# Row sums and differences made in the convolution stage, and a forward transform folded twice along x

## The chip, the cores and the metric

The kernel runs on one core of a Trainium2 chip. The metric is the device time of one launch in microseconds (us); below it is given as the median of the runs. Where a span is named, it is the time from the first to the last instruction of one profiled execution.

## The reference

The input x has 16 images of 16 channels of 256 x 256 numbers, all float32. Two layers follow each other:

```python
x = x + _L0_conv_ref(_gn(x), L0_conv_weight)
x = x + _L1_conv_ref(_gn(x), ty, tx, weights_pole1, weights_pole2, weights_residue)
```

`_gn` normalizes groups of two channels of an image to mean 0 and variance 1. The first layer is a circular 3 x 3 convolution over the 16 channels, written with Fourier transforms in the reference; v is its result with x added. The second layer is a Laplace neural operator:

```python
alpha = jnp.fft.fft2(x, axes=(-2, -1))
A = 1.0 / (omega1[:, None, None, None] - weights_pole1[None])
Bm = 1.0 / (omega2[:, None, None, None] - weights_pole2[None])
S = jnp.einsum('ikpq,oikp,xikq->oxik', weights_residue, A, Bm)
output_residue1 = jnp.einsum('biox,oxik->bkox', alpha, S)
C = jnp.einsum('biox,oikp->bikpx', alpha, A)
D = jnp.einsum('bikpx,xikq->bikpq', C, Bm)
output_residue2 = jnp.einsum('bikpq,ikpq->bkpq', D, weights_residue)
x1 = jnp.fft.ifft2(output_residue1, ...).real
...
x2 = jnp.einsum('kbiqz,biqx->kizx', F, E2).real
return x1 + x2 / Nx / Ny
```

So the spectrum alpha of each image is mixed over the channels at each frequency and transformed back (x1), and 4 x 4 projections of it onto the poles, for each image and channel, are expanded as exponentials (x2). The result is v + x1 + x2/(Nx Ny).

## The kernel before

The kernel goes through four stages; between them, data lies in scratch in HBM.

**Convolution** (order written by hand: the stage is under a manual schedule). The partitions hold four bands of 32 (r = 0 to 3) of the image's rows, each band with 2 rows times 16 channels; bands 2 and 3 hold the lower half of the image. `load_x` (L107) brings half an image as one transfer of 128 partitions, on SP's queue, into one of five buffers. `conv(g)` (L216) issues one round of 16 products of 32 x 32 (L230): four column positions c times four bands r. Six rounds make a unit u of a band, four units an image, and bands 2 and 3 run three rounds behind bands 0 and 1. When a unit is full, ACT evicts it to a buffer vt (L248, five buffers), SP stores it to vD (L252), and the sums for the group norm of the second layer are taken by ACT (L256) for odd bands and by DVE's bn_stats (L263) for even ones. Bands 2 and 3 are mirrored when they are evicted, so that the store has rows y and 255 - y side by side, lower and upper half of vD[b]. Two further strands run beside it, one step at a time: `x_stats` (L146) makes the weights and biases of the next image, with a due time for each step counted in rounds before the image starts; and the tables of the second layer (`make_hat` L319, `make_exps` L394, `make_c` L438, `make_coef` L373) are made by generators, one step every 2 or 5 rounds (L549 to L570), on all engines.

**Statistics of v.** `v_stats` (L265) runs after the last round, for all 16 images at once: DVE steps, two small products on PE, a root on ACT. It gives vmr, the mean and the inverse deviation for each image and channel.

**Forward** (L578 to L703; its order is made by the scheduler from the program's loops). A unit is one channel i and four images. `fold` (L597) loads the two halves of v with four transfers on SP (L601), makes their sum and difference s on POOL (L605, L606; 1024 elements each), and folds s along x into vf on DVE: L610 (four instructions of 128 elements, with the mean added), L613 (512) and L614 (1024). `lines` (L617) transforms along y: sixteen products of 128 x 128 x 256 (L623, L631), with vf as the weights; ACT evicts them to t, four times 768 elements (L639). `columns` (L647) makes the projections psd (L652) and the transform along x, ps_x: four products of 128 x 128 x 512 with the cosine and sine tables (L663). ACT copies the odd half to q (L666); DVE combines even and odd half into spec (L669 to L672, one input from PSUM); small parts are set by ACT (L675) and POOL (L676). After four units, spec (4096 KB) goes to aD on ACT's queue (L690), and the projections are multiplied by their coefficients on DVE (L702) and added up on POOL (L703). The pools of the stage are opened in the order b_const, vy, fold_y, fold_x, lines, sines, spec, prod.

**Mix** (L708 to L942, manual schedule). The constants ct (from cD, 4096 KB), p2k, kgrp and mcol are loaded on SP (L735 to L742); DVE makes the weights of a group (L754 to L780), POOL spreads them (L783), PE sums over poles (L805), and PE mixes channels (L863), with the spectrum loaded from aD (L849) into abd, which POOL sets to zero at first (L907). Results go to yD.

**Inverse** (L945 to L1039, order made by the scheduler). For each output channel and four images: POOL folds yk into u (L993), PE transforms back (ps_p L1018, ps_h L1007, ps_f L1023 and L1024), ACT copies the second half of ps_f to q (L1026). For each image DVE makes sum and difference r of the halves (L1028, L1029), and folds r out along x into ol (L1030, L1031, both inputs in SBUF); then it adds v, loaded as vl (L1034, 2048 elements), and the result is stored on ACT's queue.

A float32 product is two PE instructions in the profile.

Of the kernel before, what the change touches and what calls it, by code (L numbers as in the profile page):

```python
# [16 lines left out]
B = 16  # L17
# [7 lines left out]
def conv_then_laplace_kernel(ctx: ExitStack, tc: tile.TileContext, a: dict, out: bass.AP):  # L25
# [28 lines left out]
    trig = const("trig", [P, 2, P])  # L54
# [31 lines left out]
    nc.vector.tensor_copy(tabE[:, 0], trig[:, 0])  # L86
    nc.vector.tensor_copy(tabO[:, C], trig[:, 1])
# [10 lines left out]
    vp = p1.enter_context(tc.tile_pool(name="vt", bufs=5))  # L98
    sp = p1.enter_context(tc.tile_pool(name="stats", bufs=2))
    sw = p1.enter_context(tc.tile_pool(name="setup", bufs=1))  # L100
    sa = p1.enter_context(tc.tile_pool(name="v_stats", bufs=1))
# [5 lines left out]
    def load_x(b, h):  # L107
        t = xp.tile([P, 17, N + 2], FP, name="xt", tag="xt")
        nc.sync.dma_start(out=t, in_=x[b][:, 16 * h : 16 * h + 17])
        return t  # L110
# [3 lines left out]
    def load1(name, shape):  # L114
        t = wp.tile(shape, FP, name=name, tag=name)
        nc.sync.dma_start(out=t, in_=a[name])
        return t
# [3 lines left out]
    g128 = load1("g128", [P, P])  # L121
    m16 = load1("m16", [P, C])
    halves[0].append(load_x(0, 1))
    halves[1] = [load_x(1, h) for h in range(2)]
    hatT = load1("hatT", [P, 2, 3, 2, P])
    nc.sync.dma_start(out=jmat, in_=a["jmat"])
    ones = wp.tile([P, P], FP, name="ones", tag="ones")
# [18 lines left out]
    def x_stats(b):  # L146
# [4 lines left out]
        def moments(j):  # L151
            r0 = 2 * (j % 8)
            nc.vector.bn_stats(st[:, j, :], halves[b][j // 8][:, r0 : r0 + 2, 1 : N + 1])
# [58 lines left out]
    vst = sa.tile([P, B, 8, 6], FP, name="vst", tag="vst")  # L212
    sums = sa.tile([P, 2, B, 8], FP, name="sums", tag="sums")
    shift = sa.tile([P, B], FP, name="shift", tag="shift")

    def conv(g):  # L216


        for c in range(4):
            for r in range(4):  # L220
# [7 lines left out]
                q = 8 * (u % 2) + (c if r < 2 else 3 - c) + phase  # L228
# [8 lines left out]
        for r in (0, 1) if g % 6 == 5 else (2, 3) if g % 6 == 2 else ():  # L237
# [4 lines left out]
            if r % 2 == 0:  # L242
                acc["v"] = vp.tile([P, 2, 2, N], FP, name="vt", tag="vt")
            vt = acc["v"][:, r % 2]
            col = slice(2 * u + r // 2, 2 * u + r // 2 + 1)
            by_sums = {"accum_out": sums[:, 0, b, col]} if r % 2 else {}

            nc.scalar.activation(  # L248
                vt if r < 2 else vt[:, ::-1], acc[r], AF.Identity, bias=ready[b][1], **by_sums
            )  # L250
            y = 64 * r + 16 * u if r < 2 else 240 - 64 * r - 16 * u
            nc.sync.dma_start(  # L252
                out=vD[b][r // 2, y : y + 16].rearrange("(t y) c x -> (y c) t x", t=2), in_=vt
            )
# [4 lines left out]
            else:  # L259
                later.append((g + 2, vst[:, b, col.start], vt))  # L260
        while later and (later[0][0] <= g or g >= 24 * B + 2):
            _, to, vt = later.pop(0)
            nc.vector.bn_stats(to, vt)  # L263

    def v_stats():  # L265

        ms = sa.tile([P, B, 2], FP, name="ms", tag="ms")
        s = sa.tile([P, 8, B], FP, name="vs", tag="vs")
        n = 8.0 * 512
        for b in range(B):  # L270
            nc.vector.bn_aggr(ms[:, b], vst[:, b])
        m1, v1 = ms[:, :, 0], ms[:, :, 1]
        m2, v2, d, mean, mu, e = (s[:, j] for j in range(6))
# [5 lines left out]
        nc.vector.tensor_reduce(m2, sums[:, 0], AX.X, ALU.add)  # L279
        nc.vector.tensor_reduce(v2, sums[:, 1], AX.X, ALU.add)  # L280
        ts(m2, m2, 1 / n, None, ALU.mult)
        tt(d, m2, shift, ALU.add)
# [4 lines left out]
        ps = pst.tile([P, 512], FP, name="ps_stat", tag="ps_stat")  # L287
        nc.tensor.matmul(ps[:, 0:B], lhsT=g128, rhs=mean, start=True, stop=True)
        tt(e, v1, v2, ALU.add)
        nc.vector.tensor_copy(mu, ps[:, 0:B])  # L290
# [5 lines left out]
        r = sa.tile([P, 2, B, C], FP, name="vrhs", tag="vrhs")  # L296
        shape = [P, B, C]
        for j, z in enumerate((mean, e)):
# [6 lines left out]
        ps = pst.tile([P, 512], FP, name="ps_stat", tag="ps_stat")  # L305
        nc.tensor.matmul(
            ps, lhsT=ones, rhs=r.rearrange("p s b c -> p (s b c)"), start=True, stop=True
        )
        pm, pv = (ps[:, 256 * j : 256 * j + 256].rearrange("p (b c) -> p b c", b=B) for j in range(2))
# [3 lines left out]
        ts(vmr[:, 1], pm, -4.0, None, ALU.mult)  # L313
        newton(sd, var, vmr[:, 0])
        nc.vector.reciprocal(vmr[:, 0], sd)
# [3 lines left out]
    def make_hat(side):  # L319


        kcol = sw.tile([P, 2], FP, name="s_kcol", tag="s_kcol")
# [115 lines left out]
    def make_c():  # L438
# [38 lines left out]
        for k0 in range(0, C, 2):  # L477
# [31 lines left out]
            yield  # L509
            for i0 in range(0, 4, 2):  # L510
                c = sw.tile([P, 2, N], FP, name="s_c", tag=f"s_c{i0 // 2}")
# [21 lines left out]
                nc.sync.dma_start(out=cD[:, i0 : i0 + 2, k0 // 2], in_=c)  # L533
# [5 lines left out]
    ready, acc, later = {}, {}, []  # L539
# [12 lines left out]
    )  # L552
    for g in range(24 * B + 3):
        conv(g)
        b, n = divmod(g, 24)
# [18 lines left out]
    v_stats()  # L574
# [4 lines left out]
    kp = p1.enter_context(tc.tile_pool(name="b_const", bufs=1, reuse_waits="tile"))  # L579
    vp = p1.enter_context(tc.tile_pool(name="vy", bufs=3, reuse_waits="tile"))  # L580
    sp = p1.enter_context(tc.tile_pool(name="fold_y", bufs=2, reuse_waits="tile"))
    fp = p1.enter_context(tc.tile_pool(name="fold_x", bufs=2, reuse_waits="tile"))
    lp = p1.enter_context(tc.tile_pool(name="lines", bufs=2, reuse_waits="tile"))
    kpp = p1.enter_context(tc.tile_pool(name="sines", bufs=3, reuse_waits="tile"))
# [98 lines left out]
    for i in range(C):  # L683
        spec = ap.tile([P, 2, N, B], FP, name="spec", tag="spec")
        psd = pd.tile([P, B, 32], FP, name="psd", tag="psd")
        for b0 in range(0, B, 4):
            vf = fold(i, b0)
            t = lines(i, b0, vf)
            columns(i, b0, t, spec, psd)
# [487 lines left out]
```

## Time and profile before

| | us |
|---|---|
| median of three runs (3037.42 to 3043.69) | 3040.83 |
| the profiled execution | 3037.12 |
| its span | 3035.3 |

| stage | from | to |
|---|---|---|
| first convolution product to last | 27 | 669 |
| statistics of v and first lines | 669 | 690 |
| forward | 690 | 1419 (aD of the last channel issued) |
| transition to the mix | 1419 | 1464 |
| mix | 1464 | 2204 |
| inverse, with the last stores | 2204 | 3035 |

| engine | busy us | share of the span |
|---|---|---|
| PE (TensorE products) | 2826.4 | 93% |
| DVE (VectorE) | 1856.8 | 61% |
| ACT (ScalarE) | 1434.6 | 47% |
| POOL (GpSimd) | 1044.4 | 34% |

A line of the profile for a group of instructions reads: line, engine, operation, result <- inputs, shapes, number | busy time, mean duration in ns | idle time before, and what ended it. A line of the timeline has start and duration in us, engine, line, operation, result <- inputs, shape, number of instructions put together, and in brackets the idle time before it with what ended it. SPq and ACTq stand for the issue of transfers by these engines. Durations of consecutive instructions overlap a little, so the time from start to start is used where a sum is wanted.

### The profile page before, as it was taken

To read this page: it belongs to the slowest core of one execution; us is meant where nothing else is said; L and a number is where in the kernel's file an instruction comes from. 1 tells how busy PE (TensorE), PEld (TensorE's weight loads), DVE (VectorE), ACT (ScalarE), POOL (GpSimd) and SP (SyncE) were. 2 spreads that over 40 slices of the span, in tenths; PEclk is the share of its full clock that TensorE was granted. 3 is DMA by queue.
4 is the path that set the end of the run, shared out by engine and by line. 5 is a ranking of instruction groups with operands and counts; after the bars stand their busy time and mean duration, and the time that the engine had idled before them with its cause. 6 is when DMAs were issued, how large, how long until landed. Compare 5 with 4: busy or idle time off the path is not lost.

```text
span 3035.3 us, 88319 instructions
## 1 busy us (share of the span) xinstructions
PE 2826.4 (93%) x37484; PEld 2111.6 (70%) x37484; DVE 1856.8 (61%) x3616; ACT 1434.6 (47%) x2824; POOL 1044.4 (34%) x839
## 2 busy tenths in 40 slices
PE   5889888988999999997999999999579999999998
PEld 2333344555777766775778888888578989898997
DVE  6555776647555555555444444444258887888886
ACT  3546777753444444443445555555223333333333
POOL 2223342205445544543211111111044444444442
PEclk9999999998999999998999999999789999999999
DMA  6556777855455455444466766666776767676764
GB/s 248 195 181 209 247 257 253 272 173 185 162 208 197 150 208 208 156 178 174 145 189 192 195 192 194 191 192 193 221 242 224 276 229 270 236 263 241 258 227 162
DMA packets 445914, 636.85 MB, mean 210 GB/s; under 512 B 34448, under 2 KB 434192, under 8 KB 436944
## 3 DMA queue, kind: packets, MB, share of 16 engines
q1 hardware_dynamic: 375120, 488.52, 49.9%
q10 hardware_dynamic: 69888, 134.23, 11.6%
q0 software_dynamic: 512, 8.45, 1.0%
q8 instruction: 296, 4.85, 0.6%
q14 instruction: 98, 0.80, 0.1%
HBM read 353.72 MB, written 277.35 MB: 208 GB/s over the span
## 4 chain that ended last, share of the span: by engine, by line
PE 58%; issue 5%; DMA 5%; DVE 4%; POOL 1%; ACT 1%; SPq 1%; ACTq 1%; DVEq 0%; POOLq 0%
PE ps_mix L863 15%; PE ps_s L805 8%; PE ps_f L1023 6%; PE ps_x L663 6%; PE ps_p L1018 5%; PE ps_f L1024 5%; PE ps_y L623 5%; PE ps_y L631 5%; DMA out_y<-ol 3%; PE ps_h L1007 3%; DMA yD<-yt 2%; DVE ol L1031 1%; DVE ol L1034 1%; PE psd L652 1%; DVE ol L1030 1%
## 5 line engine op out<-in xcount | busy, mean ns | idle before, releaser
L863 PE MATMUL ps_mix<-abd,sg 128*64 128x128 f32 x8192 | 478.3, 275 | 36.4 <-ACT yt L928 34.8
L863 PEld LDWEIGHTS ps_mix<-abd,sg 128*64 128x64 f32 x8192 | 447.3, 137 | 88.7 <-ACT sg L923 49.4
L993 POOL TENSOR_TENSOR u<-yk 128x512 f32<-128x512 f32 x256 | 342.8, 1370 | 466.0 <-PE ps_p L1018 407.9
L230 PE MATMUL ps_conv<-xt,wc 32*32 32x512 f32 x12288 | 475.9, 623 | 29.2 <-issue 13.1
L230 PEld LDWEIGHTS ps_conv<-xt,wc 32*32 32x32 f32 x12288 | 222.9, 105 | 227.8 <-issue 141.4
L639 ACT ACTIVATE t<-ps_y,vmr 128x768 f32<-128x768 f32 x256 | 229.8, 900 | 257.0 <-PE ps_y L631 232.4
L623 PE MATMUL ps_y<-tabE,vf 128*128 128x256 f32 x1024 | 308.0, 383 | 14.7 <-DVE vf L610 10.4
L928 DVE COPY yt<-ps_mix 128x512 f32<-128x512 f32 x128 | 88.5, 692 | 380.7 <-PE ps_mix L863 212.7
L1023 PE MATMUL ps_f<-pt,inv 128*128 128x256 f32 x1024 | 318.6, 393 | 0.3
L783 POOL TENSOR_TENSOR w<-v,mcol 128x2048 f32<-128x2048 f32 x33 | 119.1, 3608 | 580.2 <-DVE v L780 576.5
L1018 PEld LDWEIGHTS ps_p<-inv,u 128*128 128x128 f32 x2048 | 289.5, 192 | 31.5 <-POOL u L996 12.0
L631 PE MATMUL ps_y<-tabO,vf 128*128 128x256 f32 x1024 | 305.6, 380 | 1.9 <-DVE vf L613 1.9
L1024 PE MATMUL ps_f<-hs,et 128*128 128x256 f32 x1024 | 304.5, 379 | 0.0
L928 ACT COPY yt<-ps_mix 128x512 f32<-128x512 f32 x384 | 221.4, 587 | 172.6 <-PE ps_mix L863 99.5
L1018 PE MATMUL ps_p<-inv,u 128*128 128x128 f32 x2048 | 291.2, 275 | 11.2 <-POOL u L996 11.2
L1026 ACT COPY q<-ps_f 128x256 f32<-128x256 f32 x256 | 95.3, 372 | 433.8 <-PE ps_f L1024 385.6
L605 POOL TENSOR_TENSOR s<-vy 128x1024 f32<-128x1024 f32 x64 | 151.7, 2370 | 418.8 <-issue 288.9
L805 PE MATMUL ps_s<-ct,w 64*32 64x256 f32 x8448 | 262.9, 383 | 17.5 <-POOL w L783 16.6
L923 ACT COPY sg<-ps_s 128x512 f32<-128x512 f32 x248 | 159.4, 645 | 198.9 <-PE ps_s L805 188.4
L248 ACT ACTIVATE vt<-ps_conv,xq 128x512 f32<-128x512 f32 x256 | 161.2, 680 | 189.2 <-PE ps_conv L230 188.7
L663 PE MATMUL ps_x<-t,trig 128*128 128x512 f32 x512 | 247.2, 605 | 0.0
L610 DVE SCALAR_TENSOR_TENSOR vf<-s,vmr 128x128 f32<-128x128 f32 x256 | 87.6, 404 | 260.9 <-PE ps_y L631 259.8
(201 smaller groups left out, 4421.1 us busy)
## 6 DMA issues: line engine op xcount, KB each, us to landing
xt<-in_x SPq DMA_DIRECT2D x32, 2193.0 KB, 9.7
vD<-vt SPq DMA_DIRECT2D x256, 256.0 KB, 3.2
vy<-vD SPq DMA_DIRECT2D x256, 256.0 KB, 4.2
aD<-spec ACTq DMA_DIRECT2D x16, 4096.0 KB, 14.1
abd<-aD SPq DMA_DIRECT2D x512, 128.0 KB, 3.3
yD<-yt SPq DMA_DIRECT2D x512, 128.0 KB, 2.8
vl<-vD SPq DMA_DIRECT2D x256, 256.0 KB, 6.3
out_y<-ol ACTq DMA_DIRECT2D x128, 512.0 KB, 6.5
```

The costliest lines, as they stand in the source:

```text
L230: nc.tensor.matmul(acc[r][32 * c : 32 * c + 32], lhsT=ready[b][0][rows, phase, tap], rhs=halves[b][u // 2][rows, q : q + 5 : 4, 2 - tap : ...
L623: nc.tensor.matmul(ps[:, xo, 0:N], lhsT=vf[:, xo, 0, j], rhs=tabE[:, 0 : i + 2 : i + 1], start=True, stop=False, skip_group_check=True,)
L631: nc.tensor.matmul(ps[:, xo, P : P + N], lhsT=vf[:, xo, 1, j], rhs=tabO[:, i : C + 1 : C - i], start=False, stop=True, skip_group_check=True,)
L639: nc.scalar.activation(t[:, :, j].rearrange("p e l n -> p e (l n)"), ps[:, :, 0:384], AF.Copy, scale=vmr[:, 0, b0 + j, i : i + 1],)
L663: nc.tensor.matmul(ps[xo], lhsT=tab, rhs=t[:, xo, j : j + 2, 0:3:2], start=True, stop=True)
L805: nc.tensor.matmul(ps[odd][32 * iq : 32 * iq + 32, ro], lhsT=w[rows, iq, kk, ro], rhs=ct[rows, iq, kk], start=True, stop=True,)
L863: nc.tensor.matmul(ps[64 * t : 64 * t + 64, j], lhsT=sg[:, f : f + 2].rearrange("p f m -> p (f m)"), rhs=abd[jq][:, :, 2 * t + cc, 2 * jj ...
L928: (nc.vector.tensor_copy if m == 3 else nc.scalar.copy)(o, src)
L993: nc.gpsimd.tensor_tensor(u[:, :, j].rearrange("p b (c n) -> p c b n", c=8), in0, in1, o)
L1018: nc.tensor.matmul(ps[:, at], lhsT=u[:, j, n], rhs=tab, start=True, stop=True)
L1023: nc.tensor.matmul(ps[:, e], lhsT=tab, rhs=pt[:, e], start=True, stop=False)
L1024: nc.tensor.matmul(ps[:, e], lhsT=et[:, 0, k, e], rhs=hs, start=False, stop=True)
```

## The change

The change has these parts:

1. The lower half's bands now hold their rows mirrored, so that bands 0, 1 and 2, 3 of a unit face each other row by row. `load_x` fills a half image with two transfers of 64 partitions each, one row apart in the buffer.
2. In the convolution stage POOL makes the sum and the difference of the two halves as soon as a unit of bands 2 and 3 is evicted: one add into a single buffer vsum, one subtract in place in vt (four buffers instead of five). These, not v's halves, are stored to vD, three rounds later. So the forward stage loads s as it is, and L605 and L606 go.
3. The statistics of v become a generator: the first twelve images are done within the convolution's last rounds, the last four in the first two units of the forward stage. The small tables' buffers move to a pool that lives on. hatT is loaded in two versions, one for each side; two table columns are loaded instead of copied; cD is stored once for a pair of channels instead of twice.
4. The forward stage has a written order. s is loaded three units ahead (the first three units on ACT's queue, the others on SP's), the next unit is folded before the present one's lines, and the columns of the unit before stand between its lines of images 0, 1 and 2, 3.
5. `fold` folds twice along x: vf as before, then vq, sums and differences of 64 columns: for the odd part on POOL, for the even part on DVE. ps_x is then eight products of 64 x 64 x 512 on four quadrants instead of four of 128 x 128 x 512. Frequencies come out with even ones first and odd ones after; the tables of the other stages are permuted to match.
6. ACT evicts lines eight times by 384 elements instead of four times by 768. The four-element copy L675 goes to DVE. aD is stored on SP's queue. The pools are opened in the order spec, fold_y, fold_1, fold_2, sines, prod, lines, b_const.
7. In the inverse stage the folding out along x is done first, with one input in PSUM, and the sum and difference of the halves afterwards for all four images at once; v's halves come out of the stored sums with a factor 0.5.

The core of the diff:

```diff
     def load_x(b, h):
-        t = xp.tile([P, 17, N + 2], FP, name="xt", tag="xt")
-        nc.sync.dma_start(out=t, in_=x[b][:, 16 * h : 16 * h + 17])
+        t = xp.tile([P, 18, N + 2], FP, name="xt", tag="xt")
+        for j in range(2):
+            rows = slice(64 * j, 64 * j + 64)
+            nc.sync.dma_start(
+                out=t[rows, 1 - j : 18 - j], in_=x[b, rows, 16 * h : 16 * h + 17]
+            )
         return t
...
+            if r == 3:
+                lo, hi = acc["v", 0], acc["v", 1]
+                both = fp.tile([P, 2, 2, N], FP, name="vsum", tag="vsum")
+                nc.gpsimd.tensor_tensor(both, lo, hi, ALU.add)
+                nc.gpsimd.tensor_tensor(lo, lo, hi, ALU.subtract)
+                folded.append((g + 3, b, u, (both, lo)))
...
+    early = v_stats(0, B - 4, lambda: pst.tile([P, 512], FP, name="ps_stat", tag="ps_stat"))
     for g in range(24 * B + 3):
         conv(g)
+        if g > 24 * (B - 4) + 8 and g % 3 == 0:
+            next(early, None)
...
-        s = sp.tile([P, 2, 4, N], FP, name="s", tag="s")
-        nc.gpsimd.tensor_tensor(s[:, 0], vy[:, 0], vy[:, 1], ALU.add)
-        nc.gpsimd.tensor_tensor(s[:, 1], vy[:, 0], vy[:, 1], ALU.subtract)
...
+        nc.vector.tensor_tensor(vf[:, 1], lo, hi, ALU.subtract)
         for j in range(4):
             nc.vector.scalar_tensor_tensor(
                 vf[:, 0, 0, j], lo[:, 0, j], vmr[:, 1, b0 + j, i : i + 1], hi[:, 0, j], ALU.add, ALU.add
             )
         nc.vector.tensor_tensor(vf[:, 0, 1], lo[:, 1], hi[:, 1], ALU.add)
-        nc.vector.tensor_tensor(vf[:, 1], lo, hi, ALU.subtract)
...
+        vq = fp.tile([P, 2, 2, 4, 2, 64], FP, name="vq", tag="vq")
+        for xo, eng in ((1, nc.gpsimd), (0, nc.vector)):
+            lo, hi = vf[:, xo, :, :, 0:64], vf[:, xo, :, :, P - 1 : 63 : -1]
+            eng.tensor_tensor(vq[:, xo, :, :, 0], lo, hi, ALU.add)
+            eng.tensor_tensor(vq[:, xo, :, :, 1], lo, hi, ALU.subtract)
+        return vq.rearrange("p e o b h x -> p e o b (h x)")
...
-            for xo, tab in ((1, sinF), (0, cosF)):
-                nc.tensor.matmul(ps[xo], lhsT=tab, rhs=t[:, xo, j : j + 2, 0:3:2], start=True, stop=True)
...
+            for h in range(2):
+                rows = slice(64 * h, 64 * h + 64)
+                for xo in range(2):
+                    to = 64 * (h ^ xo)
+                    nc.tensor.matmul(
+                        ps[xo][to : to + 64],
+                        lhsT=fold2[rows, xo],
+                        rhs=t[rows, xo, j : j + 2, 0:3:2],
+                        start=True,
+                        stop=True,
+                    )
...
+    loaded = {u: load_v(*units[u], nc.scalar) for u in range(3)}
+    vq = fold(*units[0], loaded.pop(0))
...
+    for u in range(len(units) + 1):
+        at = units[u] if u < len(units) else None
+        if at is not None:
+            now = vq
+            t = lp.tile([P, 2, 4, 3, P], FP, name="t", tag="t")
+            if u + 1 < len(units):
+                vq = fold(*units[u + 1], loaded.pop(u + 1))
+                if u + 3 < len(units):
+                    loaded[u + 3] = load_v(*units[u + 3])
+                if u < 2:
+                    next(rest)
+            for j in range(2):
+                lines(*at, now, t, j)
+        if last is not None:
...
+            done = columns(*last, spec, psd)
+        if at is not None:
+            for j in range(2, 4):
+                lines(*at, now, t, j)
...
+        if last is not None:
+            first_slots(b0, spec, *done)
+            if b0 == B - 4:
+                project(i, psd)
+                nc.sync.dma_start(
+                    out=aD[:, 2 * i : 2 * i + 2].rearrange("p r n -> p (r n)"),
+                    in_=spec.rearrange("p r f b -> p (r f b)"),
+                )
...
-                q = qp.tile([P, N], FP, name="q", tag="q")
-                nc.scalar.copy(q, ps[:, 1])
...
-                nc.vector.tensor_tensor(ol[:, :, j, 0:P], r[:, :, 0:P], r[:, :, P:N], ALU.add)
...
-            nc.vector.tensor_tensor(ol, ol, vl, ALU.add)
+                q = qp.tile([P, 2, P], FP, name="q", tag="q")
+                nc.scalar.copy(q, ps[:, :, P:N])
+                nc.vector.tensor_tensor(r[:, :, j, 0:P], ps[:, :, 0:P], q, ALU.add)
                 nc.vector.tensor_tensor(
...
+                    r[:, :, j, N - 1 : P - 1 : -1], ps[:, :, 0:P], q, ALU.subtract
                 )
...
+            nc.vector.scalar_tensor_tensor(r, vl, 0.5, r, ALU.mult, ALU.add)
+            ol = op.tile([P, 2, 4, N], FP, name="ol", tag="ol")
+            nc.vector.tensor_tensor(ol[:, 0], r[:, 0], r[:, 1], ALU.add)
+            nc.vector.tensor_tensor(ol[:, 1], r[:, 0], r[:, 1], ALU.subtract)
```

## The prediction

> **What bounds the kernel now.** I read the busy times by stage first, then one steady stretch of the forward stage on each engine, then the two transitions beside it. Columns of the first view: the stretch and its length, then busy time of PE, weight loads, DVE, ACT and POOL, the granted TensorE clock, the DMA share and GB/s.
>
> ```profile
> 28.00:669.00 641.00, 570.78 (x12634) 268.35 (x12618) 398.10 (x755) 417.73 (x873) 179.68 (x188) 0.95 0.66 223
> ...
> 690.00:1412.00 722.00, 714.62 (x3557) 503.46 (x3556) 412.77 (x917) 314.64 (x507) 349.07 (x280) 0.99 0.51 182
> 1412.00:1464.00 52.00, 30.10 (x614) 18.00 (x614) 29.41 (x85) 10.28 (x39) 27.87 (x11) 0.77 0.36 133
> ...
> 2226.00:3020.00 794.00, 790.72 (x4562) 717.39 (x4560) 644.69 (x1075) 304.79 (x758) 362.66 (x313) 1.00 0.69 242
> ```
>
> Forward (690 to 1412) and inverse (2226 to 3020) are bound by PE, 99% busy. The convolution (28 to 669) has PE at 89% and room on POOL (180 of 641). Around 1412 to 1464 no engine is full: a chain of waits. One forward unit (four images of one channel) on PE:
>
> ```profile
> 1109.75 1.88 PE L663 MATMUL ps_x<-t,trig 128*128 128x512 f32 x4
> 1111.56 0.66 PE L652 MATMUL psd<-t,hB 128*32 128x128 f32 x16
> 1112.16 1.98 PE L663 MATMUL ps_x<-t,trig 128*128 128x512 f32 x4
> 1113.98 0.59 PE L623 MATMUL ps_y<-tabE,vf 128*128 128x256 f32 x2
> ...
> 1120.45 0.59 PE L631 MATMUL ps_y<-tabO,vf 128*128 128x256 f32 x2
> 1120.89 1.02 PE L663 MATMUL ps_x<-t,trig 128*128 128x512 f32 x2
> ```
>
> By starts: ps_x 1.81 + 1.82, psd 0.60, sixteen line products to 1120.89 = 6.91; 11.14 us a unit. With gaps 722/64 = 11.2. The next two views show the same four DVE instructions, L610, beside a busy POOL (703.07) and beside an idle one (1121.09); the third shows POOL at the first place.
>
> ```profile
> 703.07 5.42 DVE L610 SCALAR_TENSOR_TENSOR vf<-s,vmr 128x128 f32<-128x128 f32 x4
> 708.41 0.68 DVE L613 TENSOR_TENSOR vf<-s 128x512 f32<-128x512 f32 x1
> 709.02 1.21 DVE L614 TENSOR_TENSOR vf<-s 128x1024 f32<-128x1024 f32 x1
> 710.15 0.47 DVE L669 SCALAR_TENSOR_TENSOR spec<-q,cols,ps_x 128x256 f32<-128x256 f32 x1
> ```
>
> ```profile
> 1121.09 1.14 DVE L610 SCALAR_TENSOR_TENSOR vf<-s,vmr 128x128 f32<-128x128 f32 x4 [5.12 <-PE ps_y L631]
> ```
>
> ```profile
> 703.11 2.35 POOL L605 TENSOR_TENSOR s<-vy 128x1024 f32<-128x1024 f32 x1 [2.28 <-issue]
> 705.42 2.40 POOL L606 TENSOR_TENSOR s<-vy 128x1024 f32<-128x1024 f32 x1
> ```
>
> 5.42 against 1.14 us: while POOL adds, DVE's two-input instructions stand; about one gets through at each POOL boundary. POOL itself loses nearly nothing (2.35 and 2.40; median 2.37).
>
> **What the Trainium skill says.** "SBUF — State Buffer", section "Who interferes with whom": a DVE instruction with two SBUF inputs and a GpSimd instruction that reads SBUF exclude each other for a whole instruction, first come first served; one SBUF input doesn't contend. The trace agrees: 5.42 against 1.14 us above, while L669 to L672, with one input from PSUM, keep 0.39 us from start to start. Same page, "Door 1: The DMA port swizzle": 64 partitions reach half of the ports, 196 against 328 GB/s at 1 MiB; its next section adds that two such transfers serialize. No load of before is so shaped, so no run here shows it. "TensorEngine Tiling (Array Packing)", section "Tiling Modes": 64x64 tiles run in parallel, four at a time, and a change of mode drains the array. The trace agrees on the overlap: 64x32 products of L805 issue 64 in 1.92 us, 30 ns each, against 216 ns for a full 256-column pass (0.431 us per pair); a drain of the size of a product doesn't show between L663 and L652.
>
> **The change part by part**, against the profiled execution, 3037.1 us (span 3035.3).
>
> 1. *Forward, PE.* ps_x: eight 64x64 products on four quadrants for four full ones, 3.63 to 1.81. PE per unit: 6.91 + 0.60 + 1.81 = 9.3.
>
> 2. *Forward, DVE.* Before, by starts: L610 x4 1.05, L613 0.61, L614 1.13, eight L669 to L672 3.14, L702 0.60 twice in four units 0.30: 6.2. Added: the second fold's add and subtract of 512 elements, priced as L613, 1.20; two four-element copies moved from ACT, 0.2. Together 7.6. POOL loses L605/L606 and gains two 512-element folds; L703, of that size, took 1.27 each. They start as DVE's difference ends, just where DVE issues its four L610, L613 and two fold instructions, all two-input. In 2.54 us two or three pass; then one or two L610 (0.4) and 1.8 remain: fold = 1.14 + 2.6 + 2.2 = 6.0 to 6.3 instead of 4.0, a loss of 2.1. POOL's sign products (0.2, two) and projection adds (1.27, two in four units) cost about 0.6 more: 10.3 us. That is over PE's 9.3: DVE becomes the bound. Ends: 9.4 (the order hides the lock) to 11.2 (all POOL time is lost). I take 10.3. The queues: SP now carries, beside the four loads of a unit, aD once in four units. aD waits for the channel's last stores, but the loads behind it are three units ahead (31 us against a landing of 4 to 7): 0; uncovered it would be up to a unit each of 16 times. ACT loses aD and the two small copies: eight evictions of 384 elements for four of 768, 0.5 each by q's 0.58 for 512, and 2 q make 5.2 us of 10.3, no bound.
>
> 3. *Into the forward stage.* Before: last product 669, statistics of v in series to 686, loads from 678, even pace only from about 703. After, twelve images' statistics lie in the convolution (POOL and DVE have room there; without it about 5 us), the last four in units 0 and 1 (6 us of DVE). The first loads go out on ACT's queue at 669.5, behind ACT's last evictions; landing about 676, first fold 6.3, first lines 682.5. Then 64 x 10.3 = 659, 6 for the statistics, 3 for the last unit's drain: last aD at 1351 instead of 1419.15. Gain 68.
>
> 4. *Out of it.* The issues that SP and DVE made before:
>
> ```profile
> 1401.76 0.33 SPq L735 DMA_DIRECT2D ct<-cD  x1
> 1402.14 0.42 SPq L737 DMA_DIRECT2D p2k<-in_pole_k  x1
> 1402.62 0.42 SPq L739 DMA_DIRECT2D kgrp<-in_kgrp  x1
> ...
> 1438.07 32.49 SPq L849 DMA_DIRECT2D abd<-aD  x20
> ```
>
> ct (4096 KB, 12.5 us), p2k and kgrp went ahead of the last aD, which was on ACT's queue, so the mix weights began at 1419.33. After, spec is the first pool of the stage and its two buffers lie where ct comes; ct waits for aD to land (11.1 us), on SP, behind aD, and p2k, kgrp, mcol are queued behind ct. DVE's weights wait for them, POOL's w and its memset of abd (13.88) for DVE. 11.1 + 1 + 12.3 = 24.4 later. Were it not so, 0.
>
> 5. *Inverse.* PE keeps its products (12.4 us a unit). DVE loses most of its two-input instructions beside L993; it is not the bound. 794/64 = 12.4, so at most the gaps go: −3.
>
> 6. *Convolution.* (a) POOL gets 64 x 2 x 2.37 = 303 us, 180 to 483 of 641, and blocks DVE's two-input table and statistics instructions, up to 2.4 each. Statistics are due 2 to 3 rounds (3 to 5 us) ahead, so few reach PE: 0 to +30, taken +6. (b) The first loads come as two 64-partition transfers. At start the queue is full:
>
> ```profile
> xt<-in_x SPq DMA_DIRECT2D x32, 2193.0 KB, 9.7
> vD<-vt SPq DMA_DIRECT2D x256, 256.0 KB, 3.2
> ```
>
> two x tiles, 4.4 MB at about 410 GB/s, 10.7 us; at the page's ratio 1.67 it is +7; an estimate; 0 to +14, taken +8. Later, x is about half of the DMA share of 0.66; times 1.67 makes 0.88, still under 1: taken +3, up to +30. (c) The sums have one buffer: add and subtract 4.7, issue, landing 3.2, give back: some 7 us, against units of 5.7 to 7 at the end: 0 to +60, taken +5. (d) Tables by DMA, hatT loaded later: 0. The stores of the sums are as many and as large as those of vt before, but issued three rounds after the eviction, on SP ahead of later x loads; x is a whole image ahead, so a wait there is covered unless (c) holds it: 0. Together +22.
>
> Sum: −68 + 24.4 − 3 + 22 = −24.6: profiled 3012.5. The profiled execution lies 3.7 under the median of the runs, so I forecast a median of 3016.
>
> **The rivals.** *PE stays the bound.* If the fixed order lets POOL's folds fall where DVE does PSUM work, a unit is 9.4: 64 x 0.9 = 58 less: 2958. For it: only 7.6 us of DVE is work. Against: the folds start together, every time. *The convolution pays* (ends slower). The mechanism is x at half width: slow x packets stand in the same rings as the stores of the sums, whose single buffer then comes back late and holds POOL, the vt buffers and the evictions. At start +14; between 350 and 600, where the share is 0.70 to 0.82, x at 1.67 would fill the DMA to 1.05, +13; a landing longer by 2 us makes the last 30 units longer by 2: +60. Together +87: 3081. It decides from a convolution 47 us longer. For it: the rings are shared, the buffer is single. Against: the share averages 0.66. *ct is early anyway*: if its load doesn't wait for aD, 3016 − 24 = 2992; against it, the place of spec. That the lines don't get the new order can't be: the order is written out.
>
> **How the numbers follow.** A measurement of this kernel tells about 0.2% (6 us) from no change. My forecast has 0.47 (own range 2990 to 3042: 0.39 faster, 0.06 same, 0.02 slower), PE-bound 0.15 and ct early 0.08 (both faster), convolution pays 0.30 (0.26 slower, 0.04 same). Faster 0.62, same 0.10, slower 0.28. Range: 2950 to 3080, from the PE-bound case to the dear convolution.
>
> **What would show it.** Step 1: starts of ps_x quadruples 1.8 us a unit. Step 2: the four L610 (new line) taking 2.5 to 3.5 instead of 1.14, DVE over 90% busy and PE near 88% in the forward stage, 10.3 us a unit. Step 3: first ps_y near 682 after a convolution's end near 669, shifted by (6). Step 4: ct issued some 11 us after the last aD. Step 6: the convolution's end between 680 and 700, first convolution product near 35, DMA share near 0.9. It would be wrong if the convolution ended past 716, or if forward units took under 9.6 or over 10.9.

## The result, and the profile after

The changed kernel takes 3127.4 us (median of four runs, 3125.28 to 3131.95) against 3040.3 before: ratio 1.0288, 95% interval 1.0270 to 1.0306. It is slower by 87 us; forecast were 3016, and 2950 to 3080 as the range. The profiled execution took 3125.28 (span 3123.5). By stage, from the starts of the instructions in both traces:

| stretch | before | after | difference | forecast |
|---|---|---|---|---|
| to the first convolution product | 27.4 | 39.4 | +12 | +8 |
| first to last convolution product | 640.6 | 774.6 | +134 | +14 |
| last convolution product to the last aD issued | 751.1 | 684.5 | −67 | −68 |
| aD issued to the first product of the mix | 44.8 | 65.7 | +21 | +24 |
| mix, first to last product | 740.6 | 740.7 | 0 | 0 |
| from there to the end | 830.8 | 818.6 | −12 | −3 |

The sum is +88, the difference of the spans. Everything outside the convolution came as forecast within 9 us; the convolution alone turned the sign. Busy time by stretch, with the columns of the table shown for before:

```profile
0.00:39.00 39.00, 1.27 (x5) 1.10 (x5) 13.89 (x37) 1.49 (x2) 0.19 (x4) 1.00 0.91 192
39.00:815.00 776.00, 605.54 (x12640) 276.36 (x12640) 498.54 (x800) 418.61 (x874) 481.27 (x314) 0.89 0.70 187
...
832.00:1498.00 666.00, 626.16 (x4100) 438.46 (x4098) 649.45 (x1198) 372.30 (x641) 234.76 (x282) 1.00 0.54 191
1498.00:1564.00 66.00, 24.06 (x584) 15.43 (x584) 25.50 (x80) 7.73 (x33) 27.58 (x10) 0.64 0.42 162
1564.00:2305.00 741.00, 705.76 (x16076) 595.48 (x16064) 333.41 (x684) 376.68 (x632) 110.66 (x34) 0.97 0.68 193
2305.00:3123.00 818.00, 792.86 (x4612) 721.81 (x4608) 481.53 (x705) 309.92 (x769) 342.23 (x320) 0.99 0.71 243
```

In the convolution no engine is full: PE 78%, DVE 64%, POOL 62% (481 us, as worked out). PE's idle time grew from 70 to 170 us and its products took 35 us more at a granted clock of 0.89 instead of 0.95. This is a stage of engines that wait for each other. In the first 39 us the DMA engines are 91% busy, as before, and move 192 GB/s instead of 351.

The forward stage is as drawn in the prediction. PE, then DVE and POOL, in one unit:

```profile
1101.40 0.66 PE L691 MATMUL psd<-t,hB 128*32 128x128 f32 x16
1101.99 1.95 PE L706 MATMUL ps_x<-t,fold 64*64 64x512 f32 x16
1103.87 0.70 PE L663 MATMUL ps_y<-tabE,vq 128*128 128x256 f32 x2
```

```profile
1101.01 1.23 DVE L645 TENSOR_TENSOR vf<-s 128x1024 f32<-128x1024 f32 x1
1102.15 3.19 DVE L647 SCALAR_TENSOR_TENSOR vf<-s,vmr 128x128 f32<-128x128 f32 x4
1105.26 0.68 DVE L650 TENSOR_TENSOR vf<-s 128x512 f32<-128x512 f32 x1
```

```profile
1102.38 1.27 POOL L655 TENSOR_TENSOR vq<-vf 128x512 f32<-128x512 f32 x1 [1.66 <-DVE vf L645]
1103.61 1.32 POOL L656 TENSOR_TENSOR vq<-vf 128x512 f32<-128x512 f32 x1
```

ps_x takes 1.88 us from start to start, for 3.63 before. The four L647 take 3.19 instead of 1.14 while POOL folds: a loss of 2.05. ("The lock" below is this: an instruction of DVE with two inputs in SBUF stands while an add of POOL reads SBUF.) DVE is 98% busy, 649 of 666, PE 94% (88 were forecast), and fifteen channels take (1498.5 − 882.4)/60 = 10.27 us a unit. Into the mix:

```profile
1498.50 0.33 SPq L791 DMA_DIRECT2D aD<-spec  x1
1509.65 0.32 SPq L823 DMA_DIRECT2D ct<-cD  x1
1510.02 0.42 SPq L825 DMA_DIRECT2D p2k<-in_pole_k  x1
...
1539.91 5.64 SPq L937 DMA_DIRECT2D abd<-aD  x7
```

ct is issued 11.15 us after aD, when aD has landed. And what PE and POOL wait for in the convolution (engine, line, what released it: us in all, times, longest):

```profile
POOL vsum L262 <- DMA vD<-vsum: 91.3, 21, 11.1
...
PE ps_conv L235 <- issue: 38.3, 17, 4.2
...
PE ps_setup L543 <- POOL s_num L534: 28.1, 5, 9.1
```

POOL stands for the landing of vsum's stores, and PE for a table input that POOL makes behind it: 28.1 us, against 0.8 before. From these I formed two theories. A: half-width loads of x fill the rings (the queues of the DMA engines), vsum's stores land late, its one buffer holds POOL, and the tables behind POOL hold PE. B: POOL's 303 us of adding are themselves the cost, by exclusive reading with DVE (B1) or because the table steps stand behind the adds in POOL's queue (B2).

### The profile page after: what moved, and what is told of

Read it like the earlier page. It is cut to its first block, busy times and chain, and to the rows that moved or that the text cites. A ratio compares the mean times of both kernels' runs of the same rounds, so it can differ in the third digit from the quotient of the medians.

```text
span 3123.5 us, 89697 instructions
## 1 busy us (share of the span) xinstructions
PE 2756.3 (88%) x38000; PEld 2049.2 (66%) x38000; DVE 2009.9 (64%) x3512; ACT 1488.5 (48%) x2953; POOL 1205.8 (39%) x967
## 5 line engine op out<-in xcount | busy, mean ns | idle before, releaser
L235 PE MATMUL ps_conv<-xt,wc 32*32 32x512 f32 x12288 | 502.5, 658 | 64.3 <-issue 38.3
L1082 POOL TENSOR_TENSOR u<-yk 128x512 f32<-128x512 f32 x256 | 317.7, 1274 | 482.5 <-PE ps_p L1107 424.5
L679 ACT ACTIVATE t<-ps_y,vmr 128x384 f32<-128x384 f32 x512 | 297.2, 581 | 205.6 <-PE ps_y L671 205.6
L663 PE MATMUL ps_y<-tabE,vq 128*128 128x256 f32 x1024 | 317.2, 392 | 42.9 <-DVE vq L656 42.8
L1116 DVE TENSOR_TENSOR r<-ps_f,q 128x256 f32<-128x256 f32 x256 | 108.3, 423 | 329.8 <-ACT q L1115 329.8
L671 PE MATMUL ps_y<-tabO,vq 128*128 128x256 f32 x1024 | 305.7, 380 | 0.0
L1107 PEld LDWEIGHTS ps_p<-inv,u 128*128 128x128 f32 x2048 | 279.6, 192 | 28.1 <-POOL u L1085 11.8
L893 PE MATMUL ps_s<-ct,w 64*32 64x256 f32 x8448 | 261.5, 382 | 39.4 <-POOL w L871 39.4
L1107 PE MATMUL ps_p<-inv,u 128*128 128x128 f32 x2048 | 281.1, 276 | 11.1 <-POOL u L1085 11.1
L663 PEld LDWEIGHTS ps_y<-tabE,vq 128*128 128x128 f32 x1024 | 184.7, 190 | 132.7 <-ACT q L719 51.2
L262 POOL TENSOR_TENSOR vsum<-vt 128x1024 f32<-128x1024 f32 x64 | 153.6, 2399 | 237.5 <-DMA vD<-vsum 91.9
```

Source lines behind the costliest of these rows:

```text
L235: nc.tensor.matmul(acc[r][32 * c : 32 * c + 32], lhsT=ready[b][0][rows, phase, tap], rhs=halves[b][u // 2][rows, q : q + 5 : 4, 2 - tap : ...
L663: nc.tensor.matmul(ps[:, 0:N], lhsT=vf[:, xo, 0, j], rhs=tabE[:, 0 : i + 2 : i + 1], start=True, stop=False, skip_group_check=True,)
L671: nc.tensor.matmul(ps[:, P : P + N], lhsT=vf[:, xo, 1, j], rhs=tabO[:, i : C + 1 : C - i], start=False, stop=True, skip_group_check=True,)
L679: nc.scalar.activation(t[:, xo, j].rearrange("p l n -> p (l n)"), ps[:, 0:384], AF.Copy, scale=vmr[:, 0, b0 + j, i : i + 1],)
L893: nc.tensor.matmul(ps[odd][32 * iq : 32 * iq + 32, ro], lhsT=w[rows, iq, kk, ro], rhs=ct[rows, iq, kk], start=True, stop=True,)
L1082: nc.gpsimd.tensor_tensor(u[:, :, j].rearrange("p b (c n) -> p c b n", c=8), in0, in1, o)
```

## The experiments

Convolution lengths are from the start of the first product to that of the last, in the profiled execution. Ratios are to the kernel before, measured beside it on the same chip.

**x_full**, the loads at full width (x lies in HBM to match, with one row more in each half image):

```diff
-        for j in range(2):
-            rows = slice(64 * j, 64 * j + 64)
-            nc.sync.dma_start(
-                out=t[rows, 1 - j : 18 - j], in_=x[b, rows, 16 * h : 16 * h + 17]
-            )
+        nc.sync.dma_start(out=t, in_=x[b][:, 16 * h : 16 * h + 18])
```

> The changed kernel with each half image of x loaded by one transfer of 128 partitions (18 rows, laid out so in HBM) instead of two of 64. Theory A (the half-width loads fill the rings, so the stores of vsum land late, its one buffer holds POOL, and the tables behind POOL hold PE): the convolution's last product falls from 814 us to about 710, the first product from 39 to 29, the total to about 3025. Theory B (POOL's 303 us of adding are themselves the cost: exclusive reads with DVE, and the table steps queued behind them on POOL): only the start gains, total about 3110.

**no_fold**, without POOL's two adds:

```diff
-                both = fp.tile([P, 2, 2, N], FP, name="vsum", tag="vsum")
-                nc.gpsimd.tensor_tensor(both, lo, hi, ALU.add)
-                nc.gpsimd.tensor_tensor(lo, lo, hi, ALU.subtract)
-                folded.append((g + 3, b, u, (both, lo)))
+                folded.append((g + 3, b, u, (hi, lo)))
```

> The changed kernel without the sums and differences in the convolution: v's halves are stored as they are, in the places of the sums (this part of the computation is left out), all else as in the changed kernel, the half-width loads too. Theory A: the buffer of vsum is gone, but the rings are as full; the convolution loses half of what it grew by, total about 3065. Theory B: POOL is as free as before, the convolution ends near 690, total about 3005.

**vsum2**, one buffer more:

```diff
-    fp = p1.enter_context(tc.tile_pool(name="v_sums", bufs=1))
+    fp = p1.enter_context(tc.tile_pool(name="v_sums", bufs=2))
...
-        om = sw.tile([P, N], FP, name="s_om", tag="s_om")
+        om = wp.tile([P, N], FP, name="s_om", tag="hatT")
```

> The changed kernel with two buffers for vsum instead of one (the table of slots moves into the place of hatT to make room). Theory A: POOL's waits for the landing of vD, 91 us in all, go; PE's waits fall by some 60, total about 3060. Theory B: the same adds in the same order, total about 3115.

**x_full_vsum2** has the first and third edit, **x_full_no_fold** the first and second.

> Both edits, full-width loads and two buffers for vsum. Theory A: the convolution ends near 690, total about 3000. Theory B: about 3100, little better than the full-width loads alone.

> Full-width loads of x, and no sums and differences in the convolution (left out: v's halves are stored in their places). If the half-width loads and POOL's adds are the whole cost, the convolution takes about 645 us from first product to last, as before the change (641), and the total is about 2980. If a third part of the change costs (tables by DMA, statistics inside the stage, a later hatT), it stays above 670 and 3005.

| kernel | median us | ratio, 95% interval | first product at | convolution |
|---|---|---|---|---|
| after | 3127.4 | 1.0288 (1.0270 to 1.0306) | 39.4 | 774.6 |
| x_full | 3060.9 | 1.0084 (1.0069 to 1.0099) | 29.7 | 724.7 |
| no_fold | 3060.2 | 1.0078 (1.0059 to 1.0096) | 39.3 | 713.5 |
| vsum2 | 3094.1 | 1.0192 (1.0177 to 1.0208) | 39.5 | 749.3 |
| x_full_vsum2 | 3058.8 | 1.0074 (1.0057 to 1.0091) | 29.1 | 720.2 |
| x_full_no_fold | 2983.5 | 0.9814 (0.9792 to 0.9836) | 29.7 | 648.7 |

Neither theory alone is right: two causes of like size nearly add up (65 and 76 us apart, 126 together). With both gone the convolution is back at 648.7, and the rest of the change wins 1.9%; that kernel leaves the sums out, so this bounds what the rest can win. Against it, the half-width loads alone (no_fold) cost 65 us and 10 at the start, the adds alone (x_full) 76. The second buffer is worth 25 us where the loads are at half width, and 5 where they are not: theory A's chain through the buffer is real, but it is not most of what the loads cost. What does the rest is seen on PE where no vsum exists, first in no_fold, then in x_full_no_fold:

```profile
PE ps_conv L235 <- issue: 60.5, 21, 5.4
...
PE ps_conv L231 <- issue: 22.6, 14, 4.0
```

These are 38 us more of waiting for which the profile names no releaser. Another 25 us are PE's products, 599.5 us busy instead of 574.3 at a granted clock of 0.90 instead of 0.95; together 63 of the 65. PE does not wait for x here, though a load of x with half the bytes lands after 12.6 us where the whole one took 10.0: in no_fold each half image had landed 27 to 98 us before PE's first product on it, as far as the trace tells landings. The trace's packets tell what ends these waits: all 21 ended 1.2 to 1.7 us after the landing of a packet of 16 KB on the queue "q8 instruction", which brought 99 packets in these 713 us; of the other products of the convolution one in ten started that soon after one. One of the waits:

```profile
673.73 1.99 PE L235 MATMUL ps_conv<-xt,wc 32*32 32x512 f32 x22 [4.72 <-issue]
```

Its packet started at 670.99 and took 1.38 us. So PE waits for instructions, and does so more when x comes at half width; how the loads hold these packets up isn't shown.

**x_full_memset** and **x_full_dve** split theory B, both from x_full_vsum2:

```diff
-                nc.gpsimd.tensor_tensor(both, lo, hi, ALU.add)
-                nc.gpsimd.tensor_tensor(lo, lo, hi, ALU.subtract)
+                nc.gpsimd.tensor_tensor(
+                    both[:, 0, 0, 0:4], lo[:, 0, 0, 0:4], hi[:, 1, 1, 0:4], ALU.add
+                )
+                for z in (both, lo):
+                    for _ in range(3):
+                        nc.gpsimd.memset(z, 0.0)
```

> Full-width loads, two buffers for vsum, and in the place of each add on POOL three memsets of the same tile (0.87 us each by the memset of abd) behind one add of four elements that keeps the wait for the eviction; the sums are left out. POOL is as long busy but doesn't read SBUF. Theory B1 (POOL's reads stop DVE's two-input instructions): the convolution falls from 720 to about 670, total about 3005. Theory B2 (POOL's queue: table steps stand behind the adds and reach PE late): nothing changes, total about 3060.

```diff
-                nc.gpsimd.tensor_tensor(both, lo, hi, ALU.add)
-                nc.gpsimd.tensor_tensor(lo, lo, hi, ALU.subtract)
-                folded.append((g + 3, b, u, (both, lo)))
+                sums_due.append((g + 2, b, u, lo, hi))
...
+            nc.vector.tensor_tensor(both, lo, hi, ALU.add)
+            nc.vector.tensor_tensor(lo, lo, hi, ALU.subtract)
+            folded.append((g + 1, b, u, (both, lo)))
```

> Full-width loads, two buffers for vsum, sums and differences made by DVE two rounds after the eviction instead of by POOL. B1 and B2 both expect the lock and the queue to go; DVE gets 64 x 2 x 1.14 = 146 us, 400 to 546 of 641. Convolution about 670, total about 3005. If DVE's load is itself on the path: 3050.

Convolutions 718.0 and 711.0, totals 3057.0 (ratio 1.0055, 1.0038 to 1.0073) and 3045.9 (1.0022, 1.0013 to 1.0031). Taking away the reads changed 2 us, though DVE's busy time fell from 501 to 431 us. (The memsets hold POOL 66 us longer than the adds did, 552 against 486, which may hide a part of a gain; no run separates this.) x_full_dve missed the 670 that B1 and B2 both expected: on DVE the adds cost 62 us, on POOL 72, near its third case, DVE's load on the path. So far B2 fitted POOL best. It makes a forecast of its own: PE must gain when the strands get more room.

**slack**, from x_full_vsum2 (its core; make_hat and the products of make_c likewise):

```diff
             nc.gpsimd.tensor_tensor(num, num, den, ALU.mult)
-            yield
-            yield
+            for _ in range(4):
+                yield
...
-        (5, 1, chain(make_exps(0), make_exps(1), make_coef())),
+        (4, 1, chain(make_exps(0), make_exps(1), make_coef())),
```

> Full-width loads, two buffers for vsum, the same adds on POOL, but the steps of the tables stand further apart: one to two generator steps more between POOL's or DVE's part and the PE or DVE part that reads it, the exponentials' strand stepped every 4 rounds instead of 5 so that it still ends in time, and the weights of an image due one round earlier. Theory B2 (PE, in its fixed order, reaches table and statistics products before POOL, delayed by the adds, has fed them): the convolution falls from 720 to about 675, total about 3010. Rival (POOL or DVE are simply too full, whatever the order): within 10 us of 3059.

Convolution 694.8, total 3032.1, ratio 0.9979 (0.9965 to 0.9993): 25 of the 72 us that the adds cost in x_full_vsum2 come back, less than the 45 expected. PE's wait for s_num is gone from the head of its list, and at its head is now PE's wait for the statistics of x (22.8 us, behind DVE). So I took the reads away once more, now with room in the tables.

**slack_memset**, slack with the memsets (and the early statistics stepped as in slack_ct2 below):

> The slack kernel (and the early statistics stepped as in slack_ct2) with POOL's adds in the convolution replaced by memsets as in x_full_memset; the sums are left out. Theory (what remains of the cost, 46 us, is the exclusive reading: statistics chains of DVE late by the length of POOL's adds): the convolution ends near 690, total about 2995. Rival (POOL's time itself is the rest): the convolution ends within 8 us of slack_ct2's, total about 3018.

The convolution is 644.6, total 2985.0, ratio 0.9832 (0.9810 to 0.9854), against 693.9 in slack_ct2, which has the same convolution with the adds. The windows from 30 us to the last product, first of slack_memset, then of slack_ct2:

```profile
30.00:674.00 644.00, 564.44 (x12638) 268.25 (x12622) 431.82 (x798) 417.74 (x872) 552.60 (x627) 0.94 0.64 226
```

```profile
30.00:723.00 693.00, 580.31 (x12637) 275.49 (x12622) 532.59 (x798) 418.23 (x872) 488.19 (x314) 0.91 0.60 211
```

POOL is busier in the faster one, 552 against 488 us: with room in the tables POOL's time as such costs nothing. Without room it does: x_full_memset, where POOL is as busy and reads as little, takes 718.0, and x_full_no_fold without this work 648.7. DVE has 798 instructions in both and takes 101 us less. So the adds hurt twice, one behind the other: while the tables have no room, PE waits for them and the lock is hidden (718.0 against 720.2); with room, the lock is what is left, 49 us (16 of them in PE's products, 580 instead of 564 us busy at a granted clock of 0.91 instead of 0.94).

**conv_before** undoes the convolution part and keeps the rest:

```diff
-        for xo, eng in ((1, nc.gpsimd), (0, nc.vector)):
+        for xo, eng in ((0, nc.vector), (1, nc.vector)):
...
+    def fold_y(vy):
+        s = sp.tile([P, 2, 4, N], FP, name="s", tag="s")
+        nc.gpsimd.tensor_tensor(s[:, 0], vy[:, 0], vy[:, 1], ALU.add)
+        nc.gpsimd.tensor_tensor(s[:, 1], vy[:, 0], vy[:, 1], ALU.subtract)
+        return s
...
-                vq = fold(*units[u + 1], loaded.pop(u + 1))
+                vq = fold(*units[u + 1], s_next)
...
+                    s_next = fold_y(loaded.pop(u + 2))
```

> All of the change but its convolution part: x layout, loads, evictions and stores as before the change; early statistics, written forward order, second fold along x (all of it on DVE) and the new inverse as after it; POOL makes sums and differences in the forward stage, one unit ahead, while DVE works on PSUM. Theory (all of the loss is in the convolution): convolution ends near 669, forward units 9.4 to 10.3 us, total about 2985. Rival (POOL's adds of 4.7 us a unit stop DVE as before): 10.8 a unit, total about 3025.

A miss: 3218.7, ratio 1.0587 (1.0564 to 1.0610). The convolution is back, 648.3, but a unit takes 13.0 us in a quiet stretch. DVE, then POOL:

```profile
1008.31 0.69 DVE L648 TENSOR_TENSOR vq<-vf 128x512 f32<-128x512 f32 x1
1008.92 2.84 DVE L649 TENSOR_TENSOR vq<-vf 128x512 f32<-128x512 f32 x1
1011.68 2.83 DVE L648 TENSOR_TENSOR vq<-vf 128x512 f32<-128x512 f32 x1
1014.43 0.68 DVE L649 TENSOR_TENSOR vq<-vf 128x512 f32<-128x512 f32 x1
1015.04 0.47 DVE L716 SCALAR_TENSOR_TENSOR spec<-q,cols,ps_x 128x256 f32<-128x256 f32 x1
```

```profile
1008.34 2.87 POOL L629 TENSOR_TENSOR s<-vy 128x1024 f32<-128x1024 f32 x1 [3.16 <-DMA vy<-vD]
1011.17 2.79 POOL L630 TENSOR_TENSOR s<-vy 128x1024 f32<-128x1024 f32 x1
```

POOL got its buffer s the moment L643 had read it (the wait of 55 of the 64 L629; the one shown waited for its load, which came at the same time), and added through the two-input folds (2.84 instead of 0.61) and not through the PSUM work that begins at 1015.04. **conv_gate_ct** moves it there by one small add that waits for the last fold; it also has ct early, as slack_ct below:

```diff
+        nc.gpsimd.tensor_tensor(gate, vq[:, 1, 0, 0, 1, 0:4], vq[:, 1, 1, 0, 1, 0:4], ALU.add)
         return vq.rearrange("p e o b h x -> p e o b (h x)")
```

> The convolution of the kernel before, sums and differences by POOL in the forward stage as in conv_before, but with one add of four elements ahead of them on POOL that waits for DVE's last fold instruction: POOL then adds while DVE works on PSUM. With ct early as in slack_ct. Theory (in conv_before POOL's adds fell on DVE's four two-input folds): a forward unit takes 10.5 us instead of 13 to 14, total about 2975. Rival (POOL's adds of 4.7 us can't be hidden behind 3.3 us of PSUM work): 12 a unit, total about 3070.

3055.2, ratio 1.0066 (1.0043 to 1.0088). A quiet unit takes 10.56 us (L639 at 1000.93 and 1011.49), the mean over fourteen channels 11.3 (13.7 in conv_before): between theory and rival. The place of POOL's adds was worth 2.4 us a unit; 4.7 us of them don't fit behind 3.3 us of PSUM work.

**The way into the mix.** slack_ct lays ct over the forward tables and puts the last aD on ACT's queue; slack_ct2 loads the small constants ahead of ct (in both the buffers of the inverse stage are reordered too; it takes 818 us as before that):

```diff
-                nc.sync.dma_start(
+                (nc.scalar if i == C - 1 else nc.sync).dma_start(
...
-    g0 = pool(p2, "sg0")
-    a0 = pool(p2, "abd0")
     kp = pool(p2, "m_const")
     up = pool(p2, "uv")
+    g0 = pool(p2, "sg0")
     wp = pool(p2, "w", 2)
+    a0 = pool(p2, "abd0")
```

> The kernel before in this list, and ct laid where the tables of the forward stage were, with the last aD on ACT's queue, so that ct, p2k, kgrp and mcol can be loaded before spec has been written out. Theory (ct's wait for spec makes the transition long): the mix starts 45 to 50 us after the last aD is issued instead of 66; total 16 to 21 less than without it. Rival (another wait of the transition takes its place, as the memset of abd that waits for spec): less than 6.

(The kernel before in this list is slack.)

> As slack_ct, with p2k, kgrp and mcol loaded ahead of ct instead of behind it, and the early statistics of v stepped so that their first product doesn't stand in front of DVE's reading of the same PSUM bank (13 us of PE's waiting once). Theory (in slack_ct the small constants landed 23 us after their issue, behind ct and aD, and the mix weights waited for them): the mix starts 48 us after the last aD instead of 61, the convolution ends 10 us earlier, total about 3003. Rival (the memset of abd or the load of the spectrum then ends last anyway): 57 us after aD, total about 3012.

From aD to the mix: slack 67.6 us, slack_ct 61.1, slack_ct2 52.0. Totals 3025.2 (0.9956, 0.9942 to 0.9969) and 3015.1 (0.9930, 0.9914 to 0.9946). slack_ct brought 6.5 us where 16 to 21 were expected. In it p2k was issued at 1402.34 and DVE had it at 1425.48; ct, issued before it, landed at 1418.63, and the last aD, issued after it on ACT's queue, at 1425.30. Issued ahead of both in slack_ct2, p2k landed after 1.74 us.

```profile
1425.48 0.19 DVE L836 TENSOR_TENSOR prU<-p2k 128x32 f32<-128x32 f32 x1 [17.28 <-DMA p2k<-in_pole_k]
```

What is left is POOL's second w of slack_ct2, which waited 8.54 us for aD, since its buffer lies over spec. The new stepping of the statistics gained nothing: 693.9 against 694.6.

**slack_ct2_vq** tests the step that came out right. The second fold is wholly DVE's:

```diff
-        for xo, eng in ((1, nc.gpsimd), (0, nc.vector)):
+        for xo, eng in ((1, nc.vector), (0, nc.vector)):
```

> As slack_ct2, with the second fold of the odd part (two instructions of 512 elements a unit) on DVE instead of POOL. Theory (in the changed kernel's forward stage DVE is the bound because POOL's two folds stop L647 for 2.1 us): DVE works 0.9 us less a unit in spite of 1.2 more of its own, PE becomes the bound at 9.4 to 9.5 instead of 10.3, total about 55 less than slack_ct2. Rival (DVE's 1.2 us more outweigh the stop): 10.6 a unit, total 20 more.

2970.4, ratio 0.9773 (0.9756 to 0.9789), the fastest here and faster than both kernels. DVE does 1.2 us more a unit and is less in the way. The stage, and its DVE in one unit:

```profile
740.00:1340.00 600.00, 596.92 (x3954) 431.61 (x3955) 582.01 (x1294) 361.32 (x622) 73.42 (x150) 0.99 0.61 215
```

```profile
1050.77 1.13 DVE L646 SCALAR_TENSOR_TENSOR vf<-s,vmr 128x128 f32<-128x128 f32 x4
...
1055.77 0.48 DVE L722 SCALAR_TENSOR_TENSOR spec<-q,cols,ps_x 128x256 f32<-128x256 f32 x1 [0.85 <-ACT q L718]
```

PE is 99% busy again, DVE waits 0.85 us, and a unit takes (1327.4 − 791.1)/56 = 9.58 us instead of 10.37.

## Why the prediction was wrong, step by step

*Steps 1 and 2, forward.* Right, in mechanism and size: ps_x 1.88 for 1.81 forecast, the lock's loss 2.05 for 2.1, a unit 10.27 for 10.3; slack_ct2_vq shows that the lock is the reason. PE's own floor was set a little low: where PE is the bound, a unit takes 9.58, not 9.3. (722/64 is 11.3, not 11.2; nothing rests on it.) *Step 3.* First lines 17.4 us after the last convolution product instead of 13.5; from there to aD 667 for 668. *Step 4.* ct 11.15 us behind aD, mix 20.9 us later for 24.4. The waits are those named, but not in the weights given: ct ahead of spec returned 6.5 us, the small constants ahead of ct 9.1 more. *Step 5.* −12 for −3. conv_before and conv_gate_ct, which add v as before the change, take 827 and 824 us there, so 6 to 8 of the 12 go with the new adding of v; the rest no run isolates.

*Step 6 failed*, in its terms (a) and (b) above all. (a) "Few reach PE", +6 taken, range to +30: the adds cost 76 us with everything else in order. I priced the lock only by how long one statistic is late, and left out that PE takes table products in a written order with little room, and that POOL's table steps now stand behind adds which themselves wait for evictions. (b) "+8 at the start, +3 later": the start was +10 to +12, but the loads cost 65 more. I reasoned from a share under 1; the share was 0.70 to 0.76, below the 0.9 expected, and the half-width loads delayed the stage all the same. What was put at nothing is what else the DMA engines bring: PE waited 38 us more for instructions, and its products took 25 us more. That x is a whole image ahead held for PE. SP did wait for PE to free a buffer of x, 64.1 us in 14 waits against 1.4 before, but this is no measure of the cost: x_full_no_fold, with its convolution of 648.7, has 182.8. The Trainium skill's "SBUF — State Buffer", section "Door 1: The DMA port swizzle" (196 GB/s for 64 partitions at 1 MiB) agrees with the 192 GB/s of the first 39 us; it stood in the prediction, which for the later loads set it against the share alone. (That two such transfers serialize stands on that page under "Can I just issue two DMAs to hit both halves?", not in the section next to it.) (c) +5: 5 where the loads are wide, 25 where they are not. (d) 0: at most 8, by which x_full_no_fold (648.7) is longer than before (640.6).

The rival that ends slower, the convolution that pays, named x at half width, the shared rings and the one buffer. These are there, but the buffer, its largest term with +60, is worth 25, and at 3081 it was 46 short; POOL's adds, 76 us, were no part of it. Its deciding point, a convolution 47 us longer, was passed by 99 (12 at the start and 134 within). Of "what would make the prediction wrong", the end of the convolution past 716 came true, at 814.

## What to carry to other kernels

Work moved into a stage with idle engines isn't free when the stage runs in a written order: price it by the slack of each consumer behind it in the same queue, and not by the busy share. On POOL, adds that read SBUF have a second price, paid by DVE's two-input instructions (four of them 3.19 instead of 1.14 us here); moving the adds to DVE can be the cheaper side (9.58 against 10.37 us a unit), or gain little (62 against 72 us in the convolution). Transfers to 64 partitions ran at about half the rate at the start here (192 against 351 GB/s): price them so wherever they occur, together with what shares the DMA engines with them, PE's instructions too.

## What was not expected of the hardware

In a stage of many small products PE waited for its own instructions: in no_fold each of the 21 waits of its convolution products without a named releaser ended 1.2 to 1.7 us after a packet of 16 KB on the queue "q8 instruction" had landed. The one edit of the loads of x moved these waits from 22.6 to 60.5 us; the profile calls them "issue" and names no more.

With the table steps tight, replacing POOL's adds by memsets changed the convolution by 2 us (718.0 against 720.2); with room, the same edit changed it by 49 (644.6 against 693.9). Of two stacked causes, removing one alone can show next to nothing. And where PE had gaps its granted clock was lower over the whole stage: 0.95 before, 0.89 after, 0.94 in slack_memset. Which of the two brings the other isn't shown.
